# Spreading group statistics over partitions: full-width matmuls before the first layer, finer ones between the layers

## The chip, the cores and the metric

The kernel runs on one core of a Trainium2 chip. The metric is the device time of one execution in microseconds (us), the median of several runs. A core has five engines that work side by side and wait for each other by semaphores: TensorE (PE, matrix multiplication, with its weight loads shown apart as PEld), VectorE (DVE), ScalarE (ACT), GpSimd (POOL) and SyncE (SP, which here only issues DMA transfers). TensorE multiplies a stationary operand (the weights, loaded first) with a moving operand whose columns are streamed through, and writes to PSUM, from where the other engines fetch the result.

## The reference

Two layers, each a group normalization over the whole of the other axes, then a convolution whose weights differ for each batch and position, made by a small network from `z`, and a residual:

```python
def _gn(v, G=32, eps=1e-5):                 # v: (S2=32, B=32, CI=64, L=256)
    B_, H_, W_, C_ = v.shape
    g = v.reshape(B_, H_, W_, G, C_ // G)   # 32 groups of 8 positions
    m = jnp.mean(g, axis=(1, 2, 4), keepdims=True)
    s = jnp.var(g, axis=(1, 2, 4), keepdims=True)
    return ((g - m) / jnp.sqrt(s + eps)).reshape(v.shape)

def _L0_conv_ref(x, z, W1, b1, g1, be1, W2, b2, Wb1, bb1, gb1, beb1, Wb2, bb2):
    h = jax.nn.relu(_ln(z @ W1 + b1, g1, be1))
    w = (h @ W2 + b2).reshape(B, L, CI, CO, K)
    hb = jax.nn.relu(_ln(z @ Wb1 + bb1, gb1, beb1))
    bias = (hb @ Wb2 + bb2).transpose(0, 2, 1)
    ...                                     # x padded by 1, three shifted views
    out = jnp.einsum('sbilk,bliok->sbol', x_uf, w)
    return out + bias[None]

x = x + _L0_conv_ref(_gn(x), ...)
x = x + _L1_conv_ref(_gn(x), ...)           # the same with other parameters
```

There is one mean and one deviation for each of 32 samples and 32 groups: 1024 pairs of numbers in a layer. All is float32.

## The kernel before

First, in one phase, the hidden activations of both small networks are made and the statistics of `x` are taken (VectorE, `bn_stats`). Then for each of 128 half batches (64 batches of two layers, two halves of the output channels) TensorE makes the convolution weights (`make`), VectorE and ScalarE take them out of PSUM and add `b2` (`take`), and TensorE applies them to the normalized input (`products`).

The statistics are computed with partition p = 32 t + s for a quarter t of the positions and a sample s: each partition holds the 8 groups of its quarter. But the normalization needs all 32 groups of all 32 samples on every one of 128 partitions. This is done in two steps. `diagonals` puts each number on a diagonal: `gmean[p, (t, g), s]` is the mean where p = 32 t + s, else 0. `spread` multiplies by a matrix of ones, so that every partition receives the sum over partitions, which has a single term that isn't 0:

```python
def diagonals():
    m, v = prep[:, 0], prep[:, 1]
    nc.scalar.activation(v, v, AF.Sqrt, bias=eps)                          # L377
    nc.vector.reciprocal(v, v)                                             # L378
    one = ident.rearrange("p (t s) -> p t s", t=NT)
    shape = [P, NT, GT, S]
    for g in range(GT):                                                    # 8 times
        nc.scalar.activation(                                              # L382
            gmean.rearrange("p (t g) s -> p t g s", t=NT)[:, :, g], one, AF.Copy, scale=m[:, g : g + 1]
        )
    nc.vector.tensor_tensor(rstd..., one..., v..., ALU.mult)               # L385

def spread():
    for to in (gmean, rstd):                                # each [128, G=32, S=32]
        ps = ps_g.tile([P, G, S], FP, tag="pg", name="spread")
        for h in range(2):
            hs = slice(h * G // 2, (h + 1) * G // 2)
            for r in range(0, P, C):                        # C = 64: halves of the array
                nc.tensor.matmul(                                          # L399
                    ps[r : r + C, hs], ones[:, r : r + C], to[:, hs, :], start=True, stop=True
                )
        nc.scalar.copy(to, ps)                                             # L402
```

In a matmul's form in the profile, `128*64 128x512` is 64 columns of weights on 128 partitions, and a moving operand of 512 columns. Two matmuls with outputs on partitions 0 to 63 and 64 to 127 use the two halves of the array. The weights of the convolution are made in the same manner, from the same three PSUM buffers (`ps_g`, tag `pg`):

```python
def make(h, kind, o0):
    pg = ps_g.tile([P, OG, M], FP, tag="pg", name="pg")
    ...
    for k in range(OG):
        w = w2[:, o0 + k, :]
        nc.tensor.matmul(pg[0:C, k, :], w[:, k0 * C : (k0 + 1) * C], h0, start=True, stop=True)  # L484
        nc.tensor.matmul(pg[C:P, k, :], w[:, k1 * C : (k1 + 1) * C], h1, start=True, stop=True)  # L485
    return pg
```

`take` evicts them by VectorE (line 496) and, for one kind in three, half by ScalarE in eight pieces (line 507). The two places where the statistics are spread:

```python
    first_phase(first_weights)
    ...
    batches(first_parts, B)              # VectorE: statistics of the first layer
    diagonals()
    spread()
    for k in range(9, len(order)):       # the last three of twelve weight tiles
        weights(0, k)                    # make and take
    normalize_first(0, nc.vector)        # reads gmean and rstd            # L471
    next_pairs(1, 0)

    for v in range(1, NH * U):
        for k in range(len(order)):
            weights(v, k, False, (lambda: products(v - 1)) if k == 0 else None)
            if k == 0:
                after(v - 1)             # at v = 64: last_batch(), diagonals()
            if v == NH * B and k == 3:   # between the layers
                spread()
                normalize_first(B, nc.gpsimd)
                next_pairs(B + 1, 0)
```

The order of instructions on each engine is that of the program. In the first phase, full-width transposes (line 204: `nc.tensor.transpose(p2[...], hs[...], ident)`) stand among 64-column matmuls (lines 176 and 221).

## Time and profile before

| | |
|---|---|
| median of three runs | 4170.51 us (4169.96 to 4175.55) |
| span of the profiled execution | 4172.1 us |
| mean granted TensorE clock | 0.973 |
| spread before the first layer | 316.13 to 321.37 us |
| spread between the layers | 2244.93 to about 2248.7 us |

The profile is of one execution. Its page gives each engine's busy time, then the chain of waits that ended last: from the last instruction back, at each step to what released it. Groups of instructions are named by line, engine, operation and tile; `x` is their count. A timeline lists instructions in order of time, with the start, the duration, and in brackets the idle time before and what ended it. What lies beside that chain can grow by its slack without moving the end; what lies on it counts in full.

### The profile page before, as it was taken

Reading aid. Unit: us, or ns where it says so; the run is one execution under the profiler, and the core shown is the slowest. Engines: PE = TensorE matmul, PEld = TensorE weight load, DVE = VectorE, ACT = ScalarE, POOL = GpSimd, SP = SyncE. Lnnn points to the kernel's source line nnn. Section 1 sums busy time; section 2 is a strip of 40 time slices with the busy share of each in tenths; the row PEclk is TensorE's granted clock in tenths of the full one; section 3 lists DMA queues with packets and bytes.
Section 4 is the critical chain, followed back from the end, with each engine's and each line's share of the span. In section 5 each row is a group of like instructions: output and inputs, shape, how many; then the busy total and the mean of one; then the engine's idle time right before and its main releaser. Section 6 shows DMA issues by size and latency. Waiting matters only on the chain.

```text
span 4172.1 us, 194718 instructions
## 1 busy us (share of the span) xinstructions
PE 3942.0 (94%) x91040; PEld 3737.7 (90%) x91040; DVE 2600.9 (62%) x2934; ACT 1334.4 (32%) x4480; POOL 1943.0 (47%) x638
## 2 busy tenths in 40 slices
PE   6878999999999999999999999999999999999999
PEld 3448999999999999999988999999999999999999
DVE  5576666666666666666665565655565555555565
ACT  4562332323232323233223232323232332323232
POOL 3435543554355435534534644554455445445542
PEclk8569999999999999999999999999999999999999
DMA  8876777777777777777676444544454444444343
GB/s 307 312 273 178 174 191 171 194 169 192 170 194 170 194 167 192 172 179 183 177 177 194 147 156 135 166 127 157 135 166 127 154 137 146 147 135 157 126 150 91
DMA packets 654877, 718.55 MB, mean 172 GB/s; under 512 B 567378, under 2 KB 584052, under 8 KB 585588
## 3 DMA queue, kind: packets, MB, share of 16 engines
q1 hardware_dynamic: 627060, 692.59, 58.6%
q8 instruction: 711, 11.65, 1.2%
q10 hardware_dynamic: 27008, 13.51, 1.1%
q14 instruction: 98, 0.80, 0.1%
HBM read 492.08 MB, written 213.91 MB: 169 GB/s over the span
## 4 chain that ended last, share of the span: by engine, by line
PE 86%; DVE 6%; issue 3%; DMA 2%; POOL 1%; ACT 1%; ACTq 1%; SPq 0%; DVEq 0%; POOLq 0%
PE pg L484 49%; PE pc L530 23%; PE pg L485 11%; DVE wall L496 3%; DVE parts L244 2%; PE p L176 1%; PE p L204 1%; DVE room L540 1%; DMA room<-in_xs_dram 1%; ACTq L235 1%; POOL xn L471 1%; DMA wall<-in_xs_dram 1%; DMA bd<-xn 0%; POOL xn L453 0%; PE p L221 0%
## 5 line engine op out<-in xcount | busy, mean ns | idle before, releaser
L484 PE MATMUL pg<-hT,w2t 128*64 128x128 f32 x24576 | 2740.3, 273 | 31.5 <-DVE wall L496 12.9
L485 PE MATMUL pg<-hT,w2t 128*64 128x128 f32 x24576 | 2740.1, 273 | 11.9 <-issue 11.6
L484 PEld LDWEIGHTS pg<-hT,w2t 128*64 128x64 f32 x24576 | 2684.1, 137 | 59.2 <-DVE wall L496 25.2
L485 PEld LDWEIGHTS pg<-hT,w2t 128*64 128x64 f32 x24576 | 2684.4, 137 | 16.3 <-issue 16.0
L496 DVE TENSOR_TENSOR wall<-pg,b 64x1024 f32<-64x1024 f32 x1527 | 1854.6, 1220 | 703.5 <-PE pg L485 699.1
L507 ACT ACTIVATE wall<-pg,b 64x128 f32<-64x128 f32 x4168 | 1188.8, 478 | 2672.6 <-DVE wall L496 1987.2
L453 POOL TENSOR_TENSOR xn<-room,gmean 128x2048 f32<-128x2048 f32 x124 | 572.5, 4617 | 1839.5 <-PE pc L530 1812.4
L530 PE MATMUL pc<-wall,xn 128*32 128x128 f32 (+2 forms) x40960 | 993.1, 253 | 101.7 <-issue 87.1
L530 PEld LDWEIGHTS pc<-wall,xn 128*32 128x32 f32 x40960 | 935.7, 110 | 166.4 <-issue 151.4
L540 DVE TENSOR_TENSOR room<-pc,room 128x512 f32<-128x512 f32 x512 | 353.9, 691 | 725.8 <-PE pc L530 657.6
L453 POOL TENSOR_TENSOR xn<-xn,rstd 128x2048 f32<-128x2048 f32 x124 | 653.9, 5274 | 9.7
L420 POOL TENSOR_TENSOR room<-room,bt 128x2048 f32<-128x2048 f32 x128 | 587.3, 4588 | 122.5 <-DMA bt<-bd 67.5
L244 DVE BATCH_NORM_STATS2 parts<-room 128x6 f32<-128x256 f32 (+1 forms) x592 | 241.4, 453 | 8.7
L187 POOL TENSOR_TENSOR xn<-xn 128x512 f32<-128x512 f32 (+2 forms) x192 | 103.8, 541 | 156.0 <-ACT xn L179 143.5
L204 PEld LDWEIGHTS p<-ident,xn 128*128 128x128 f32 x256 | 47.7, 208 | 89.7 <-issue 69.1
L176 PE MATMUL p<-wc,zt 17*64 17x256 f32 x512 | 111.3, 605 | 13.3 <-DVE wc L155 12.7
L204 PE MATMUL p<-ident,xn 128*128 128x128 f32 x256 | 69.3, 438 | 53.7 <-DVE xn L196 43.6
L176 PEld LDWEIGHTS p<-wc,zt 17*64 17x64 f32 x512 | 51.9, 210 | 70.8 <-issue 68.7
L244 DVE BATCH_NORM_STATS2 parts<-wall 128x6 f32<-128x512 f32 x160 | 97.8, 678 | 12.8 <-DMA wall<-in_xs_dram 12.8
L193 DVE RECIPROCAL var<-var 128x8 f32<-128x8 f32 x32 | 6.5, 202 | 108.7 <-ACT var L190 108.7
L206 ACT ACTIVATE xn<-p,vec 128x512 f32<-128x512 f32 x64 | 46.3, 774 | 22.7 <-PE p L204 22.7
L179 ACT ACTIVATE xn<-p 128x1024 f32<-128x1024 f32 x32 | 32.5, 1016 | 35.0 <-PE p L176 34.9
(58 smaller groups left out, 235.0 us busy)
## 6 DMA issues: line engine op xcount, KB each, us to landing
bt<-bd SPq DMA_DIRECT2D x512, 256.0 KB, 6.7
room<-in_xp_dram SPq DMA_DIRECT2D x64, 1024.0 KB, 9.5
room<-in_xs_dram SPq DMA_DIRECT2D x64, 1024.0 KB, 8.8
x<-room SPq DMA_DIRECT2D x64, 1024.0 KB, 5.3
x1p<-room SPq DMA_DIRECT2D x512, 128.0 KB, 6.8
room<-x1p SPq DMA_DIRECT2D x64, 1024.0 KB, 8.3
room<-x SPq DMA_DIRECT2D x64, 1024.0 KB, 8.1
out_dram<-room SPq DMA_DIRECT2D x64, 1024.0 KB, 4.8
```

What stands on the lines that cost most here:

```text
L176: nc.tensor.matmul(self.p1[r : r + C, k], self.zt[:, a : a + C], self.t["wc"], start=True, stop=True)
L187: nc.gpsimd.tensor_tensor(to, self.sq[:, :, 0:w], self.sq[:, :, w : 2 * w], ALU.add)
L204: nc.tensor.transpose(p2[:, net, k * P : (k + 1) * P], hs[:, 2 * k + net, :], ident)
L244: nc.vector.bn_stats(out, y.rearrange("p o (a m) -> p o a m", a=2)[:, :, :, g * e : (g + 1) * e])
L420: nc.gpsimd.tensor_tensor(y, y, bts.pop(v), ALU.add)
L453: nc.gpsimd.tensor_tensor(o, i, b.to_broadcast(list(o.shape)), op)
L484: nc.tensor.matmul(pg[0:C, k, :], w[:, k0 * C : (k0 + 1) * C], h0, start=True, stop=True)
L485: nc.tensor.matmul(pg[C:P, k, :], w[:, k1 * C : (k1 + 1) * C], h1, start=True, stop=True)
L496: nc.vector.tensor_tensor(place(rows, a), pg[rows].rearrange("p o (t m) -> p t m o", t=NT), b2[n][rows, kind, None, None, o0 : o0 + OG].to ...
L507: nc.scalar.activation(place(rows, a)[:, :, :, k], pg[rows, k].rearrange("p (t m) -> p t m", t=NT), AF.Identity, bias=b2[n][rows, kind, o0 ...
L530: nc.tensor.matmul(pc[t * S : (t + 1) * S, n0 - q * EB : n1 - q * EB, :], xn[:, u % 2, t * MT + p + 1, :], wall[:, t, a : a + (n1 - n0) * CH],
L540: nc.vector.tensor_tensor(part, pc.rearrange("p (m a) o -> p o a m", a=2), part, ALU.add)
```

## The change

`spread` receives, for each of the two tensors, into how many chunks n its 32 groups are cut, and how many columns w of the array a matmul uses. Before the first layer it is 2 chunks at the full width of 128 columns: four matmuls in place of eight. Between the layers it is 8 chunks for the mean and 4 for the reciprocal deviation, at 64 columns: 16 + 8 = 24 matmuls in place of eight, each over 128 or 256 moving columns instead of 512. Before the first layer TensorE has nothing else to do then, and full width needs the fewest instructions; between the layers TensorE is in a stream of small half-width matmuls, and the finer pieces have the form of this stream. What is computed is the same.

```diff
-    def spread():
-
-        for to in (gmean, rstd):
+    def spread(*how):
+
+        for to, (n, w) in zip((gmean, rstd), how):
             ps = ps_g.tile([P, G, S], FP, tag="pg", name="spread")
-            for h in range(2):
-                hs = slice(h * G // 2, (h + 1) * G // 2)
-                for r in range(0, P, C):
-                    nc.tensor.matmul(
-                        ps[r : r + C, hs], ones[:, r : r + C], to[:, hs, :], start=True, stop=True
-                    )
+            for k in range(n):
+                gs = slice(k * G // n, (k + 1) * G // n)
+                for r in range(0, P, w):
+                    nc.tensor.matmul(ps[r : r + w, gs], ones[:, r : r + w], to[:, gs], start=True, stop=True)
             nc.scalar.copy(to, ps)
@@
         diagonals()
-        spread()
+        spread((2, P), (2, P))
         for k in range(9, len(order)):
@@
-                    spread()
+                    spread((8, C), (4, C))
                     normalize_first(B, nc.gpsimd)
```

## The prediction

> **What bounds the kernel now.** I read the page first, for which engine is full, then the instructions that the change replaces, then the chain of waits and the timeline around the two places where they run. The first part of the page gives busy time, share of the span and instruction count by engine:

> ```profile
> PE 3942.0 (94%) x91040; PEld 3737.7 (90%) x91040; DVE 2600.9 (62%) x2934; ACT 1334.4 (32%) x4480; POOL 1943.0 (47%) x638
> ```

> TensorE is the bound, 94% of 4172.1 us. The question is then how much of that 94% the change touches. The answer for the source line of the spread (line 399) lists its forms:

> ```profile
> L399 PE MATMUL spread<-gmean,ones x16: 592/852/1115, 316.1 to 2246.3; 128*64 128x512 f32 x16
> L399 PE MATMUL spread<-rstd,ones x16: 592/592/641, 319.6 to 2248.0; 128*64 128x512 f32 x16
> ```

> The program issues 8 such matmuls for each tensor (4 in each of two calls) and the trace holds 16: an f32 matmul leaves two records. So the change touches 32 of 91040 records, in two places, one at 316 us and one at 2245 us. In the timeline of the first place (start, duration, engine, line, operation):

> ```profile
> 316.13 0.29 PEld L399 LDWEIGHTS spread<-gmean,ones 128*64 128x64 f32 x4 [11.07 <-ACT gmean L382]
> 316.13 3.68 PE L399 MATMUL spread<-gmean,ones 128*64 128x512 f32 x8 [10.82 <-ACT gmean L382]
> ...
> 319.60 1.93 PE L399 MATMUL spread<-rstd,ones 128*64 128x512 f32 x8
> ...
> 321.37 0.27 PE L484 MATMUL pg<-hT,w2t 128*64 128x128 f32 x1
> ```

> The two halves do equal work, yet the first takes 319.60 - 316.13 = 3.47 us and the second 321.37 - 319.60 = 1.77 us: TensorE had stood idle for 10.82 us and starts at half clock. The weight loads show the rhythm: they come in twos, at 317.04, 317.90 and 318.75, 0.85 us apart. So the two 64-column matmuls of a pair run side by side, one on each half of the array, and one pair of records takes 0.85 us at half clock, 0.43 us at full.

> The chain of waits for the first place (start, duration, what):

> ```profile
> 313.75 2.34 ACT gmean L382 x8
> 316.09 0.04 issue
> 316.13 5.40 PE spread L399 x16
> ```

> Here the spread is on the path: ScalarE makes the diagonals, TensorE spreads them, then makes weights, and VectorE normalizes. Whatever changes in these 5.40 us moves the end. The same view for the place between the layers:

> ```profile
> 2247.41 1.22 ACT wall L507 x5
> 2248.63 0.03 issue
> 2248.67 0.72 ACT wall L507 x2
> 2249.39 0.01 issue
> 2249.40 1.01 ACT gmean L402
> ```

> Here no spread matmul is on the path. The copy out of PSUM (line 402) stands behind eight weight evictions (line 507) in ScalarE's program order, and these wait for VectorE.

> [...] 3.5 us at a granted clock of 0.50 from 316.0, 0.95 in the 1.9 us after. [...] Here 64 columns take 137 ns at full clock and 128 columns 224 ns in the median, in a stage mostly at half clock[...].

> **First layer: 8 half-width matmuls become 4 full-width ones.** Removed: 4 pairs in time, each two records deep, so 8 slots of 512 columns. Added: 4 matmuls of 128x128 weights over 512 columns, two records each, so also 8 slots of 512 columns. What is a full-width record's slot? The transposes of line 204 are full width: a run of 8 over 128 columns starts at 111.04 and the next operation starts at 112.91, so at most 1.87 / 8 = 0.23 us each for 128 columns at half clock. Four times the columns is at most 0.93 us, near the 0.85 of a half-width pair; the surplus is mostly the seam (below). I choose equal slots. Then 4 slots at half clock and 4 at full clock:

> 4 x 0.853 + 4 x 0.427 = 5.12 us, before and after.

> The gain in instruction count is nothing if the slot is set by the columns streamed. The idle gaps of the weight loads, 0.62 us, show that loading isn't what fills the slot.

> New is one change of tiling: the spread now runs on the whole array, and the weight matmuls of line 484 after it on halves. Entering costs nothing, since TensorE is idle until 316.13 anyway. [...] Two seams measure it at half clock. The eight transposes would take 8 x 0.213 = 1.71 us and the next operation comes after 1.87, so 0.16. Eight 256-column pairs of line 176, at 0.427 each, start at 121.25, and full-width transposes follow at 124.94: 3.69 - 3.41 = 0.28. At full clock half of it, 0.08 to 0.14 us. I take +0.1 us, on the path.

> **Between the layers: 8 matmuls become 16 + 8.** For the mean: 8 chunks of 128 columns by two halves; for the reciprocal deviation: 4 chunks of 256 columns by two halves. Streamed are again 1024 columns of each tensor on both halves. A 128-column pair of records is just what the weight matmuls of lines 484 and 485 are, and these start every 0.11 us (321.37, then 321.48). So the mean takes 8 x 2 x 0.11 = 1.76 us against 4 x 0.427 = 1.71, and the deviation 4 x 2 x 0.215 = 1.72 against 1.71. The sum is +0.06 us on TensorE. No tiling changes here, as its neighbours also use halves. There are 16 more program matmuls, 32 records in 91040.

> None of it is on the path. In the table of stretches TensorE is nearly empty from 2248.7 to 2249.5 (0.07 us busy of 0.80), waiting for ScalarE to free PSUM; so there is 0.8 us of slack behind the spread, and the mean's product is complete some 2.5 us ahead of the copy that reads it at 2249.40. The value of this part is 0.0 us.

> **Sum.** 4170.51 + 0.1 + 0.0 = 4170.6 us. I predict 4170.6.

> **Rivals.**
> 1. *Full width is faster.* Were the two halves of a pair taking turns rather than running together, full width would halve 5.12 us and gain some 2.6 us: 4168. Against it: 0.85 us at half clock for 512 columns agrees with 0.213 us for 128 columns in the full-width transposes. Clearly less likely.
> 2. *Full width is slower.* The weight load of 128 columns could stay exposed between records, at 0.22 us each for 7 loads: +1.5 us, 4172. Against it: the loads lie under matmuls that stream 0.43 to 0.85 us. [...]
> 3. *Finer matmuls become a wait.* If each of the 24 cost a fixed price beyond its columns, say 0.1 us, TensorE would end 1.6 us later, eat the 0.8 us of slack and delay the next weights by 0.8 us. But TensorE waits soon after for GpSimd's normalization (4.0 us in total), so even this would be hidden mostly. 4171 at most.
> 4. *Finer lets the copy start earlier.* Chunks could begin after half of the diagonals. Against it: the copy stays one instruction over the whole tensor, and ScalarE reaches it at 2249.40 whatever TensorE does. No gain.

> **Range and chances.** All of the rivals lie within 3 us, less than 0.1% of the time. The width comes from the repetitions: 4169.96, 4170.51 and 4175.55 us for the same kernel. One of three lies 5 us up, so a median could too; below, 4 us for rival 1 and a luckier phase of the clock. Range 4166 to 4176. 2% is 83 us, sixteen times the 5.4 us that the first spread takes, so removing it altogether would not reach it: within 2% 0.99, 0.005 on either side.

> **What would show it.** In the profile after, line 399's successor should have full-width records 128x512, started 0.85 us apart at first and 0.43 later, and the first weight matmul of line 484 some 5.3 us after the first spread record, against 5.24 before. If that distance is under 4 us, rival 1 holds; over 6 us, rival 2. Between the layers, the records of the mean should start 0.11 us apart, the chain should still pass from the evictions of line 507 to the copy without TensorE, and the copy should start at the same distance after the last eviction. Wrong I would be by a spread that appears on the chain there, or by a change of more than 5 us, which would have to come from outside these two places, as from a shifted clock or a transfer met in another phase.

## The result

The changed kernel takes 4098.15 us in the median of four runs (4092.12 to 4100.1) against 4170.24 (4168.12 to 4175.55): ratio 0.9823, 95% interval 0.9806 to 0.984. The prediction was 4170.6, in a range from 4166 to 4176. The 72 us that were gained are more than thirteen times what the first spread takes in all, so they can't have come from the two spreads.

First part of the changed kernel's page, as it was shown for the kernel before:

```profile
PE 3927.3 (96%) x91064; PEld 3737.5 (91%) x91064; DVE 2602.2 (64%) x2934; ACT 1337.8 (33%) x4480; POOL 1946.6 (48%) x638
```

All engines but TensorE are busy as long as before. TensorE has 24 more records, less busy time by 15 us, and a span (4089.9 us) shorter by 82. It stood idle for 230 us before, now for 163.

**The two spreads.** Line 399 in the timeline of the first place:

```profile
316.81 3.78 PE L399 MATMUL spread<-gmean,ones 128*128 128x512 f32 x4 [10.82 <-ACT gmean L382]
317.82 0.34 PEld L399 LDWEIGHTS spread<-gmean,ones 128*128 128x128 f32 x1 [0.52 <-issue]
...
320.38 3.13 PE L399 MATMUL spread<-rstd,ones 128*128 128x512 f32 x4
...
322.09 0.34 PEld L399 LDWEIGHTS spread<-rstd,ones 128*128 128x128 f32 x1 [0.52 <-issue]
...
323.44 0.32 PE L482 MATMUL pg<-hT,w2t 128*64 128x128 f32 x1
```

From the first record to the first weight matmul it takes 323.44 - 316.81 = 6.63 us, against 5.24 before: longer. And the chain of waits in the second place:

```profile
2223.32 1.26 ACT wall L505 x5
2224.57 0.00 issue
2224.58 0.72 ACT wall L505 x2
2225.30 0.01 issue
2225.31 1.01 ACT gmean L400
```

It passes from the evictions to the copy as before, without TensorE. So neither spread explains a gain.

**Where the time went.** I cut both traces at the start of the products (line 530 before, 528 after) of chosen half batches, which I count from 0. The piece up to half batch 2 is longer by 3.4 us. From there to half batch 61, layer 1 takes 1738.7 us in place of 1763.2 (-24.5). From 66 to 126, layer 2 takes 1740.4 in place of 1799.4 (-59.0). The stretch between the layers gives -3.0 and the end +1.1; the sum is, but for rounding, the -82.2 us between the two spans. Nearly all of the gain lies in 119 half batches in which not one instruction was changed.

What differs there is shown by the table of waits (engine and line, what it waited for: us in total, times, longest). Before:

```profile
DVE room L540 <- PE pc L530: 657.6, 481, 6.5
PEld pc L530 <- issue: 151.4, 308, 3.0
...
PE pc L530 <- issue: 87.1, 148, 2.8
```

After:

```profile
DVE room L538 <- PE pc L528: 583.6, 479, 6.7
...
PEld pc L528 <- issue: 83.9, 228, 2.7
...
PE pc L528 <- issue: 37.8, 72, 2.5
```

VectorE waits 74 us less for the products, and TensorE's weight loads in the products stand 67.5 us less in "issue", time in which the engine waited for nothing that the profile shows. One half batch of the kernel before, TensorE's timeline:

```profile
1797.25 4.39 PE L530 MATMUL pc<-wall,xn 128*32 128x32 f32 x188
1802.72 3.22 PE L530 MATMUL pc<-wall,xn 128*32 128x128 f32 x128 [1.07 <-issue]
1806.46 0.26 PE L530 MATMUL pc<-wall,xn 128*32 128x32 f32 x4 [0.53 <-issue]
```

The 320 records of the products break after 188 and after 188 + 128. Another one, in layer 2 (half batch 112):

```profile
3709.67 2.04 PE L530 MATMUL pc<-wall,xn 128*32 128x32 f32 x88
3712.50 3.23 PE L530 MATMUL pc<-wall,xn 128*32 128x96 f32 x128 [0.79 <-issue]
3715.97 2.42 PE L530 MATMUL pc<-wall,xn 128*32 128x128 f32 x104 [0.24 <-issue]
```

Again 128 apart. The same half batch in the changed kernel breaks after 192, and at its end:

```profile
3641.30 4.41 PE L528 MATMUL pc<-wall,xn 128*32 128x32 f32 x192
3645.90 3.07 PE L528 MATMUL pc<-wall,xn 128*32 128x128 f32 x128 [0.19 <-issue]
3649.65 0.32 PE L482 MATMUL pg<-hT,w2t 128*64 128x128 f32 x1 [0.67 <-issue]
```

So it is throughout: in both traces every one of the gaps over 0.3 us between starts of successive product records (69 and 94 in the two layers before, 44 and 32 after) stands within 1.5 records of one row of places 127.955 records apart, in each layer. 128 matmul records with 128 weight loads are 256 instructions. The DMA part of the page lists two queues of instructions; the line of the larger one (packets, MB, share of 16 engines) is the same before and after:

```profile
q8 instruction: 711, 11.65, 1.2%
```

**The theory.** A half batch has 704 records, five and a half blocks, so the block boundaries stand at nearly the same place in all even half batches of a layer, and 64 records on in the odd ones (they drift by about a record in four half batches). The change makes TensorE's program 16 instructions shorter ahead of layer 1 and 64 longer between the layers, so it shifts the boundaries by -16 instructions in layer 1 and +48 in layer 2. Where they fall decides how often the fetch comes late. The rivals: the finer pieces between the layers bring the gain (A), or the full-width spread does, by clock or tiling (B).

### The profile page after: what moved, and what is told of

The parts are those of the page before. It is cut to its first block, busy times and chain, and to the rows that moved or that the text cites. A ratio compares the mean times of both kernels' runs of the same rounds, so it can differ in the third digit from the quotient of the medians.

```text
span 4089.9 us, 194766 instructions
## 1 busy us (share of the span) xinstructions
PE 3927.3 (96%) x91064; PEld 3737.5 (91%) x91064; DVE 2602.2 (64%) x2934; ACT 1337.8 (33%) x4480; POOL 1946.6 (48%) x638
## 2 busy tenths in 40 slices
DMA packets 654877, 718.55 MB, mean 176 GB/s; under 512 B 567378, under 2 KB 584052, under 8 KB 585588
## 4 chain that ended last, share of the span: by engine, by line
PE 88%; DVE 6%; DMA 2%; issue 2%; ACT 1%; POOL 1%; ACTq 1%; SPq 0%; DVEq 0%; POOLq 0%
PE pg L482 50%; PE pc L528 23%; PE pg L483 12%; DVE wall L494 2%; DVE parts L244 2%; PE p L176 2%; PE p L204 1%; DMA room<-in_xs_dram 1%; DVE room L538 1%; POOL xn L469 1%; ACTq L235 0%; DMA bd<-xn 0%; PE p L221 0%; DMA hd<-xn 0%; ACT xn L179 0%
## 5 line engine op out<-in xcount | busy, mean ns | idle before, releaser
L528 PE MATMUL pc<-wall,xn 128*32 128x128 f32 (+2 forms) x40960 | 974.2, 253 | 50.8 <-issue 37.8
```

What stands on the lines that cost most here:

```text
L528: nc.tensor.matmul(pc[t * S : (t + 1) * S, n0 - q * EB : n1 - q * EB, :], xn[:, u % 2, t * MT + p + 1, :], wall[:, t, a : a + (n1 - n0) * CH],
```

## The experiments

Ratios are to the kernel before, on the same chip in the same session, with the 95% interval; its median differed between the sessions (4165 to 4189 us), so times of different sessions are compared by ratio only. A ratio stands as recorded with the runs and can differ from the quotient of the two medians by up to 0.0014. "Stall" is the sum of distances between starts of successive product records that are over 0.3 us, in place of the usual 0.02; "stretch" is the piece from half batch 2 to 61 (layer 1) or 66 to 126 (layer 2). An idle matmul is four instructions that change no result:

```diff
+            for _ in range(pad if to is gmean else 0):
+                nc.tensor.matmul(ps[0:C, 0:1], ones[:, 0:C], ones[:, 0:S], start=True, stop=True)
```

**One half of the change at a time.**

```diff
-                    spread((8, C), (4, C))
+                    spread((2, C), (2, C))
```

> Only the full-width spread before the first layer is taken over; between the layers stands the old spread. It shortens TensorE's instruction stream by 16 instructions (4 matmuls of 2 weight loads and 2 multiplications each) from the first layer on. Theory (where the instruction stream is cut into fetched blocks of 256 instructions decides the time): layer 1 runs as in the changed kernel, about 22 us sooner at the second spread than before; layer 2 then stands at a position that no run has shown, so in all 4120 to 4165 us. Rival A (the finer pieces between the layers bring the gain): 4170 to 4173, as the first spread itself is up to 2 us longer. Rival B (the full-width spread, by clock or tiling, brings the gain): 4098.

Measured 4161.85 us, ratio 0.9966 (0.995 to 0.9981). Layer 1's stretch is 1741.6 us, as in the changed kernel, with a stall of 36 us in place of 59; layer 2's is 1800.9, as before. The full-width spread alone gives a fifth to a quarter of the gain (0.34% of 1.77% by the ratio, 21.6 of 82 us by the stretch), and gives it in layer 1.

```diff
-        spread((2, P), (2, P))
+        spread((2, C), (2, C))
```

> Only the finer spread between the layers is taken over. Layer 1 is instruction for instruction that of the kernel before; the stream is 64 instructions longer from layer 2 on (16 more matmuls of 4). Theory (fetched blocks): the second spread starts at 2245 us as before, layer 2 gains some 40 to 60 us, in all 4110 to 4130. Rival A (finer pieces bring the gain by the chain at the spread itself): 4098. Rival B (the full-width spread brings it): 4170.

Measured 4119.61 us, ratio 0.9853 (0.9836 to 0.987). Layer 1 takes 1767.6 us and layer 2 1737.8. Each half acts on the layer behind it, and the two together (0.34% and 1.47%) make up the whole (1.77%). Neither rival alone gives both.

**The old spreads with the new shifts.**

```diff
-        spread((2, P), (2, P))
+        spread((2, C), (2, C), pad=60)
-                    spread((8, C), (4, C))
+                    spread((2, C), (2, C), pad=16)
```

> The kernel before with both spreads in their old form. Only idle matmuls are put ahead of them, which write 32 columns of PSUM that the spread overwrites: 60 ahead of the first, while TensorE waits anyway, and 16 ahead of the second. This shifts the instruction stream by +240 and then +304 instructions, which is -16 and +48 modulo a block of 256, as in the changed kernel. Theory (fetched blocks): 4092 to 4106 us, though more work is done. Rivals A and B (the forms of the spread): 4170 to 4173.

Measured 4108.02 us (4100.24 to 4111.08), ratio 0.9824 (0.9804 to 0.9844), the ratio of the changed kernel, without either of its spreads. The time itself lies 2 us above what was expected, which the session accounts for: the kernel before stood at 4181.71. Its waits:

```profile
PEld pc L530 <- issue: 94.6, 234, 3.2
```

The stretches are 1746.1 and 1740.5 us. The 60 idle matmuls, from 310.51 us on, put the first spread off to 323.12 us (316.13 before), and half batch 2 starts 11.3 us later than before; the gain bears that too.

**The new spreads with the old shifts.**

```diff
-        spread((2, P), (2, P))
+        spread((2, P), (2, P), pad=4)
-                    spread((8, C), (4, C))
+                    spread((8, C), (4, C), pad=48)
```

> The changed kernel, with 4 idle matmuls ahead of its first spread and 48 ahead of the second, so that its instruction stream stands again as in the kernel before, modulo a block of 256 (-16+16 = 0 in layer 1, 0+64+192 = 256 in layer 2). Theory (fetched blocks): the gain is gone, 4166 to 4178 us. Rivals A and B: 4098 to 4102.

Measured 4186.22 us, ratio 1.0015 (1.0 to 1.003): the gain is gone, in the same session. Above the expected range by the session again. Stretches of 1762.6 and 1791.3, and

```profile
PEld pc L530 <- issue: 147.4, 305, 2.3
```

against 151.4 and 308 before. This pair settles which of the two it is: the gain goes with the shift, not with the forms. An effect of the forms below the 8 us by which stretches at the same shift differ (1746.1 and 1738.7, 1791.3 and 1799.4) isn't excluded.

**Other shifts.** The old spreads, with idle matmuls ahead of them:

```diff
+        spread((2, C), (2, C), pad=20)     # 12, 24
+                    spread((2, C), (2, C), pad=16)     # 12, 16
```

> The kernel before, both spreads in their old form, with 20 and 16 idle matmuls ahead of them: the instruction stream is shifted by 80 instructions in layer 1 and by 144 in layer 2. In the six traces so far, the stretch from the third to the last but two half batch of layer 1 took 1739 to 1768 us, and 1738 to 1801 us in layer 2, by the shift. Theory (position of the fetched blocks in the products): the time depends on the shift alone, in either layer a value between about 1715 and 1805 us; with the other parts of the time as before, 4080 to 4190 in all. Rival (only the particular shifts of the changed kernel, or its forms, have an effect): 4170 to 4185.

> As the last, with 12 and 12 idle matmuls: shifts of 48 in layer 1 and 96 in layer 2. Shift 96 lies 32 beyond the 64 of the finer spread alone (1738 us in layer 2), so a smooth dependence would give 1730 to 1765 there. Shift 48 in layer 1 is 64 beyond the changed kernel's -16: anything between 1715 and 1805. Rival: 4170 to 4185.

> As the last, with 24 and 16 idle matmuls: shifts of 96 in layer 1 and 160 in layer 2. Two half batches are 11 blocks and a few instructions, and one is five and a half; so a shift by 128 only exchanges odd and even half batches. Shift 96 then stands 16 before the changed kernel's -16 (= 112 + 128), and if the dependence is smooth layer 1 takes about 1740 or less. Layer 2 at 160 stands like 32, between the 0 and 48 that took 1797 and 1740: 1745 to 1790. Rival: 4170 to 4185.

Measured 4157.85, 4145.23 and 4158.98 us, ratios 0.9917 (0.989 to 0.9944), 0.9888 (0.9844 to 0.9932) and 0.9916 (0.9889 to 0.9943). Layer 2 is fast in all (1745.2, 1740.6, 1735.1), layer 1 slower than before in all (1792.8, 1793.0, 1803.4). The third misses what I expected, layer 1 at 1740 and layer 2 at 1745 to 1790: odd and even half batches can't be exchanged, so the full 256 instructions count.

**A search by the table so found.** Idle matmuls at the very start, where TensorE waits for its first input, and finer pieces between the layers:

```diff
+        ps = ps_g.tile([P, G, S], FP, tag="pg", name="idle")
+        for _ in range(58):                # 52, 42, 30
+            nc.tensor.matmul(ps[0:C, 0:1], ones[:, 0:C], ones[:, 0:S], start=True, stop=True)
         first_phase(first_weights)
@@
-                    spread()
+                    spread((8, C), (8, C))     # (16, C), (8, C) twice; (4, C), (2, C)
```

> The last runs showed the dependence on the shift to differ between odd and even half batches: with the first block boundary of an even half batch's products at record 74 to 109 (of 128) layer 1 took 1793 to 1803 us and layer 2 1791 to 1801, at 5 and 14 layer 1 took 1763 and 1740, and at 17 to 72 layer 2 took 1735 to 1745. Here 52 idle matmuls stand at the very start, where TensorE waits for its first input, and the spread between the layers is cut into 16 and 8 chunks: boundaries at 31 in layer 1 and about 42 in layer 2. Theory (position): both layers 1730 to 1750, in all 4080 to 4105. Rival (layer 1 has its best near the changed kernel's 14 and is slow elsewhere): layer 1 at 1760 or more, 4115 or more in all.

> As the last with 42 idle matmuls: boundaries at 51 in layer 1 and about 62 in layer 2. Theory: both layers 1730 to 1750, 4080 to 4105 in all. Rival: layer 1 at 1760 or more.

> As the last with 58 idle matmuls and 8 chunks for both tensors between the layers: boundaries at 19 in layer 1, next to the changed kernel's 14, and about 62 in layer 2. Theory and rival both: layer 1 at 1735 to 1750, layer 2 at 1738, 4085 to 4105 in all, level with the changed kernel.

> As the last with 30 idle matmuls and 4 and 2 chunks between the layers: boundaries at 75 in layer 1, where layer 2 took 1740, and about 30 in layer 2. If layer 1 follows the same curve as layer 2: 1735 to 1750 and 4085 to 4110 in all. If layer 1's slow range, seen from 85 on, begins earlier: 1770 or more, 4120 or more in all. Layer 2 in either case 1735 to 1745.

Measured 4103.27, 4116.12, 4082.97 and 4149.06 us; ratios 0.9846 (0.9824 to 0.9867), 0.9877 (0.9857 to 0.9896), 0.9799 (0.9781 to 0.9817) and 0.9963 (0.9949 to 0.9976). Layer 2 is fast four times; layer 1 has a narrow good place, missed by b1 and b2 a little and by b4 wholly. At the boundaries of b2 and b4 layer 1 takes 1765.7 and 1799.5 us, as the rival view had it; b1's 1755.0 lies between the two views, though its whole time is in the theory's range. Layer 1 doesn't follow layer 2's curve. b3 is the best version seen; its interval overlaps that of the changed kernel's 0.9823, and they were not run side by side, so that it beats the changed kernel isn't shown.

The 13 kernels so far together, ordered by the record (of 128) at which the first boundary of an even half batch's products stands some ten half batches into the layer, read from the stalls to about one record:

| boundary | layer 1 stretch, us | boundary | layer 2 stretch, us |
|---|---|---|---|
| 5 | 1763.2, 1767.6, 1762.6 | 17 | 1735.1 |
| 14 | 1738.7, 1741.6, 1746.1 | 25, 29 | 1745.2, 1732.8 |
| 18 | 1736.0 | 40, 49 | 1734.3, 1740.6 |
| 30 | 1755.0 | 61 | 1727.3, 1727.5 |
| 50 | 1765.7 | 65 | 1737.8 |
| 74 | 1799.5 | 72, 73 | 1740.4, 1740.5 |
| 85 | 1803.4 | 97, 98 | 1799.4, 1791.3 |
| 94, 109 | 1792.8, 1793.0 | 105 | 1800.9 |

Kernels with different spreads and the same boundary (5, 14, 61, 72 and 73, 97 and 98) agree within 8.1 us, and different boundaries of one layer differ by up to 74. The kernel before stood at 5 and 97.

**Fewer and larger data packets beside the fetches.** The kernel before, with layer 1's transposed copy written in 8 KB pieces (131608 DMA packets in all in place of 654877, with the same bytes):

```diff
-            for k in some:
-                t, a = divmod(k, 2)
+            if 0 in some:
+                to = x1p[u][h * C : (h + 1) * C]
                 nc.sync.dma_start(
-                    out=x1p[u][a * C + h * CH : ...].rearrange("o s m -> s o m"),
-                    in_=residual(v)[t * S : (t + 1) * S, :, a * MT : (a + 1) * MT],
+                    out=bass.AP(to.tensor, to.offset, [[CH * LT, P], [1, CH * LT]]),
+                    in_=residual(v).rearrange("p o l -> p (o l)"),
                 )
```

> The kernel before without idle matmuls; the transposed copy of layer 1's result that layer 2 reads, stored in pieces of 128 bytes, is replaced by one store for each half batch of the same bytes in pieces of 8 KB, so that layer 2 reads its input in the wrong order. TensorE's program is unchanged. Theory with a second part (the fetches are late because they queue behind data transfers): the stall within the products of layer 1, 59 us before from the third half batch on, falls to 35 or less, while layer 2, which stores no such copy, keeps its 66. If the fetch is slow by itself, layer 1 keeps 55 to 60 and the stretch its 1763 us.

Measured 4165.55 us, ratio 0.9934 (0.9909 to 0.9958), with a layer 2 that reads its input in the wrong order. The boundaries are where they were. The row of DMA's busy share in 40 slices, before and here, shows the lighter layer 1 (0.58 of the engines from 396 to 2160 us, 0.73 before):

```profile
DMA  8876777777777777777676444544454444444343
DMA  8875565656565556565555544444454445444442
```

The stall in layer 1's products falls from 59 to 15 us, its stretch from 1763 to 1741 us; the weight matmuls get 20 us of other gaps. Layer 2 keeps a stall of 68 us. So, with the same program of TensorE and the same boundaries, the stall in the products depends on the data transfers beside it. The traces show where: just one fetch ends between two successive boundaries, and it is its start that moves, not its length. For boundaries within layer 1's products it starts 1.06 us (median) after the boundary before, and 0.33 here; the fetches of the layer take 1.05 us before and 1.12 here. With the 1.40 us from its end to the next record, the sum is 0.33 + 1.12 + 1.40 = 2.85 us, about the 2.83 in which a block is used up; before it was 3.51. In the changed kernel the start is at 0.74 us in layer 1 and 0.36 in layer 2 (1.12 before). What makes a fetch start late isn't shown. The shorter stretch may have a second cause: VectorE no longer waits for the copy's stores, 63.6 us before.

## Why the prediction was wrong

By its own steps:

- *"The question is then how much of that 94% the change touches ... 32 of 91040 records, in two places."* This is the step that failed. An instruction inserted moves every later one against the fetched blocks (the first boundary of an even half batch's products went from record 5 to 14 in layer 1 and from 97 to 72 in layer 2), so the change touched all of the products. The value of "16 more program matmuls" was put at 0.0 us; with the 16 instructions saved ahead of layer 1 it is -24.5 us in layer 1 and -59.0 in layer 2, and with idle matmuls in their place (e3) the same ratio comes out, 0.9824.
- *Idle time of TensorE.* I read its busy share, and not what its idle time consisted of. The line "PE pc L530 <- issue: 87.1" stood in the waits of the kernel before: over a third of the 230 us that TensorE was idle, in the bounding engine, with no engine to blame. The rivals were about two places, and none was about this.
- *First spread: equal slots.* Right: at a granted clock of 0.50 full-width loads come 0.85 us apart (317.82, 318.68, 319.53), as the pairs did. The +0.1 us for leaving full width was right too: the first weight matmul starts 0.52 us after the last full-width record in all three kernels that have them, and 0.43 us after the last pair in the kernel before. Entering wasn't free: the first record takes 1.01 us, the first pair 0.91. What was off is the clock: in the trace's record of it a granted clock of 0.50 lasts until 319.7 us before and 322.9 after, 3.6 and 6.1 us from the first spread record, and so the spread takes 6.63 us instead of 5.3. Over the 14 traces it is 2.8 to 6.1 us, whatever the spread, so the 4 x 0.853 = 3.41 us that the prediction's sum has at half clock are no constant here. And the 6.63 us, over the 6 that the prediction set as a sign of its rival 2, don't prove it: in four kernels with half-width spreads the distance is over 6 us too (6.27 to 6.50).
- *Between the layers: nothing on the path.* Right for the place itself, as the chain shows. The mean's records took 1.97 us in all against 1.94 before, and the next tensor's began 1.77 us after the first instead of 1.74.
- *"Wrong I would be by ... a change of more than 5 us, which would have to come from outside these two places."* So it was. The prediction named the case, with "a transfer met in another phase" as the nearest of its guesses, but gave it no room: the range was taken from repetitions of one and the same program. Repetitions have the same boundaries and can't show what moving them does. (And 83 us are fifteen times the 5.4 us of the first spread, not sixteen.)

What stays open: why a boundary at 74 is bad in layer 1 (1799.5 us) while 72 and 73 are good in layer 2 (1740), and why 30 and 50 cost 20 to 30 us in layer 1 alone. The stall depends on data transfers (59 to 15 us in layer 1 by m1), and the layers' transfers differ; which transfer meets which fetch, and how it puts off the fetch's start, wasn't tried.

## What to carry to other kernels

In a long unrolled program, look at TensorE's idle time put down to "issue": gaps 128 matmul records apart were here read as instruction fetches that came late, in stretches that used up 256 instructions in 2.83 us while fetches started 3.28 us apart or more. This kernel's time changed by up to 2% (ratio 0.9799 in b3) when instructions were added ahead, so before a small gain or loss is credited to an edit, repeat it with idle instructions that restore the old position. A chosen shift only tunes one build. Larger data packets beside the fast stretch went with a stall of 15 us in place of 59 in layer 1's products in m1; whether fewer, larger instructions in it would help too, no run tried.

## What the runs showed of the hardware that was not expected

The 16384-byte packets of the queue `q8 instruction` started 3.23 to 3.31 us apart at the least in fourteen kernels (3.28 in the kernel before), while 128 records of the changed kernel's fastest products took 2.83 us. With 16 instructions fewer ahead of it, layer 1's stretch was 24.5 us shorter (1738.7 us in place of 1763.2).

An idle matmul of 32 columns, many in a row on the same half of the array, took 0.107 us per record ahead of the first spread of e3, at a granted clock of 0.50, and 0.058 us ahead of the second, at 1.00: more than twice the 0.022 to 0.027 of product records, which alternate over four groups of 32 columns. And the 12.6 us of idle matmuls in e3, in which TensorE counts as busy throughout, passed at a granted clock of 0.50 to the end; it rose to 1.00 at 327.5 us, 4.4 us into the spread behind them.
